# Layer 1 of a two-layer AdaLN model in smaller portions per tick, with longer lags, states in three groups and fewer experts summed ahead

## The chip, the cores and the metric

The kernel runs on one core of a Trainium2 chip. The metric is the device time of one execution in microseconds; lower is better. Engines are named as the profile names them: PE (TensorE), DVE (VectorE), ACT (ScalarE), POOL (GpSimd) and SP (SyncE, which here only issues DMAs).

## The reference, cut to what matters

Eight batches of 512 tokens with 128 channels pass through two blocks. Each half of a block normalises the tokens, scales and shifts them by a vector per batch, applies a sublayer and adds its gated result to `x`.

```python
h = layernorm(x) * (1 + ca0) + sa0;  x = x + ga0 * attention(h)          # Layer 0: 16 heads of 8
h = layernorm(x) * (1 + cb0) + sb0;  x = x + gb0 * moe(h)                # 8 experts 128-512-128, top 2, and a shared one
h = layernorm(x) * (1 + ca1) + sa1;  x = x + ga1 * ssm(h)                # Layer 1, first half
h = layernorm(x) * (1 + cb1) + sb1;  x = x + gb1 * ffn(h)                # Layer 1, second half

def ssm(x):            # 16 states
    xc = conv(x, 4 taps along tokens, per channel) + conv_b
    delta, B_in, C = split(xc @ Win + b_in)          # B_in and C: means of pairs
    A = -exp(A_log);  dA = softplus(delta) * A;  A_bar = exp(dA)
    B_bar = (A_bar - 1) / A * B_in                   # a Taylor form where A is tiny
    h = scan(h * A_bar + B_bar along tokens)
    return (C * h) @ Wout + b_out

def ffn(x):
    x1 = x + silu(pointwise(conv(x, 3 taps)) + pw_b)
    rw = softmax weights of the top 2 of x1 @ router
    combined = sum over 8 experts of rw[e] * silu(x1 @ expert_w[e] + expert_b[e])
    h = rmsnorm(x1 + combined @ out_w + out_b) * norm_w
    return h + gelu(h @ down) @ up
```

## The kernel before, in words

All data are float32; one matmul of the program is two passes on PE. `x` of each batch stays in SBUF as `xs[b]`, 128 tokens on partitions by four chunks (`NC4`).

**Attention** runs in half-ticks called slots (`slot(s)`), with other work hung on slots by `at_slot`. Layer 0's tokens are scattered to DRAM rows sorted by expert (`x_rows`) while attention runs.

**Layer 0's experts** run in a loop of `n = 62` ticks, one block of 256 rows a tick: 31 routed blocks of batches 0-5, 12 blocks of the shared expert, 15 routed blocks of batches 6-7, 4 shared ones. In tick i the loop does `turn_in` of block i+1 (PE transposes, DVE copies to `xt`), `up` of block i (`ph`, L943, then four Gelus on ACT), `down` of block i-1 (`pyb`, L954), and the fetches of blocks ahead: rows `xg` and first weights `w1b` three blocks ahead (`fetch`), second weights `w2b` two ahead (`fetch_2`). Results go to DRAM (`y_rows`).

**Layer 1** is a list of events: `when(t, do, ...)` appends a call to tick t, and a tick's calls are issued in the order in which they were appended. Events of ticks below n run inside the expert loop, after that tick's block; the ticks from n on have no blocks, and follow one another. All engines but PE's matmuls inside a helper are wrapped so that they keep program order, and PE's matmuls are pinned too, so every engine executes in the order in which the ticks issue.

Per batch, the first half of Layer 1 consists of: `gather` (16 indirect DMAs on POOL fetch a batch's two expert results per token in pieces, L974), `combine` (DVE adds them by gate, adds to `xs[b]`, and takes statistics), `ssm_root` (a power on POOL), `ssm_centre` (DVE ends the root, ACT writes the centred tokens `xh`, POOL adds a bias row to `xs[b]`), `ssm_channels` (PE transposes `ptn`, L1107, ACT scales), `ssm_conv` (DVE, into `xc`, two buffers). `ssm_project(h, s)` brings two batches' states on 32 partitions (`pj`, L1146); `chain_1` to `chain_4` compute the softplus, the exponentials and the scan for a group of batches at once, with 16 partitions per batch; `ssm_out` brings them back (`py`, L1214).

Before the change there are two groups of four batches. Batches 0-5 take these steps in ticks 36-51, inside the loop; group 0's chain has ticks 48-53. Batches 6 and 7 take them in ticks n+1 to n+8, and group 1's chain starts at n+10.

The second half begins with the lead-in of a batch, 12 calls from `ssm_out` to `ffn_gates_out`: statistics, root, centre, channels, `ffn_pointwise` (`pw`, L1240, then Silu to `sl`, which shares the two buffers of `xc`), router logits, ranks, gates, and the gates' way to DRAM. From there `ffn_spread` broadcasts them to all partitions (`gb`). Then come eight experts a batch, one a tick: `expert_in` (PE `pe`, L1334, and Silu on ACT to `ye`), three ticks later `expert_gate` (DVE multiplies by the gate into `t`), sums of `t` (two or four by POOL, all eight by DVE in `all_eight`), `expert_sum` (PE multiplies by `out_w`, `r`, L1322). `rms_squares`, `rms_root`, `rms_scale`, `rms_turn` normalise and transpose, `ff_down` and `ff_up` finish for batches 0-3, 4-6 and 7. A batch's first expert is at tick `base[b] = n + 2 + 8b`.

Single-bank PSUM tiles (`bank`) have four buffers, two-bank tiles (`pair`, which `ph` and `r` use) two.

Of the kernel before, what the change touches and what calls it, by code (L numbers as in the profile page):

```python
# [19 lines left out]
P = 128  # L20
# [48 lines left out]
def tile_adaln_two_blocks(  # L69
# [288 lines left out]
    with tc.tile_pool(name="at", bufs=2) as at, tc.tile_pool(name="sc", bufs=4, space=PSUM) as psc, tc.tile_pool(  # L358
# [22 lines left out]
        def load_batch(b, step):  # L381
# [10 lines left out]
            else:  # L392
# [4 lines left out]
                ht = ate.tile([P, S], FP, tag="ht", name="ht", bufs=2)  # L397
# [443 lines left out]
        def routed(h, i):  # L841


            def fetch(it):
# [11 lines left out]
                it["xg"] = fr.tile([P, 2, D], FP, tag="xg", name="xg", bufs=3)  # L856
                Q.dma_start(out=it["xg"], in_=x_rows[h][bass.ds(r, BLK), :].rearrange("(c p) d -> p c d", p=P))
                it["w1"] = fr.tile([P, NF * P], FP, tag="w1b", name="w1b", bufs=3)
                Q.dma_start(out=it["w1"], in_=w1t[:, bass.ds(e, 1), :].rearrange("p o f -> p (o f)"))
# [8 lines left out]
            def turn_in(it):  # L868
                ps = bank("pxt")
                for c in range(2):  # L870
                    pin(T.transpose(ps[:, c, :], it["xg"][:, c, :], ident))  # L871
                it["x"] = fw.tile([P, BLK], FP, tag="xt", name="xt")
                V.tensor_copy(it["x"], flat(ps)[:, 0:BLK])

            def leave(it, py):
# [7 lines left out]
                "fetch": fetch,  # L883
                "fetch_2": fetch_2,
# [6 lines left out]
        def everyone(b, i):  # L891
# [11 lines left out]
            def turn_in(it):  # L903
# [4 lines left out]
                it["gt"] = fw.tile([NE + 1, BLK], FP, tag="gt", name="gt", bufs=3)  # L908
# [15 lines left out]
            def leave(it, py):  # L924
# [5 lines left out]
                "fetch": fetch,  # L930
                "fetch_2": lambda it: None,
# [50 lines left out]
        def combine(b):  # L982
            h, j = home(b)
            acc, yg = shared[b], gathered.pop(b)
            for c in range(NC4):
                n = NC4 * j + c
                for k in range(2):
                    V.scalar_tensor_tensor(
                        acc[:, c, :], yg[:, k, c, :], half[h]["gates"][:, k, n : n + 1], acc[:, c, :], ALU.mult, ALU.add
                    )  # L990
            V.tensor_tensor(acc, acc, sb_rows[:, b : b + 1, :].to_broadcast([P, NC4, D]), ALU.mult)
            V.tensor_tensor(xs[b], xs[b], acc, ALU.add)
            stats(xs[b], mv3, b)
# [78 lines left out]
        def pointwise():  # L1072
# [7 lines left out]
            V.tensor_add(pwb, pp[:, 0:1], col("pw_b"))  # L1080

# [30 lines left out]
        GB = B // 2  # L1112
        GR = 32 * GB // 2

# [3 lines left out]
        def ssm_centre(b):  # L1118
            held["xh", b] = centre(b, mv3, rs3, held.pop(("v3", b)))
            G.tensor_tensor(xs[b], xs[b], gab_rows[:, b : b + 1, :].to_broadcast([P, NC4, D]), ALU.add)  # L1120
# [4 lines left out]
        def ssm_conv(b):  # L1125
            hp, n = held.pop(("hp", b)), S - 1
            xc = lt([P, S], "xc", bufs=2)
            G.memset(xc[:, n:S], 0.0)
            V.tensor_scalar(xc[:, 0:n], hp[:, 0:n], col("conv_w", 0), col("conv_b"), ALU.mult, ALU.add)
            for k in range(1, 4):  # L1130
                V.scalar_tensor_tensor(
                    xc[:, 0:n], hp[:, k : k + n], col("conv_w", k), xc[:, 0:n], ALU.mult, ALU.add
                )
            held["xc", b] = xc

        def ssm_project(h, s):

            if s == 0:
                for name in ("dl", "bi", "ci"):
                    held[name] = lt([GR, S], name)  # L1140
            ps = flat(bank("pj"))
            for i in range(2):
                xc = held.pop(("xc", h * GB + 2 * s + i))
# [13 lines left out]
        def chained(name, tag=None):  # L1157
            held[name] = lt([GR, S], name, tag=tag)
            return held[name]

        def of_states(name, i=0):
            return k1[name][0:GR, i : i + 1]

        def chain_1(h, step):

            dl = held["dl"]
            if step == 0:
                V.tensor_scalar(dl, dl, of_states("bias"), None, ALU.add)
                u = chained("u")
                V.scalar_tensor_tensor(u, dl, -1.0, dl, ALU.mult, ALU.min)  # L1170
            else:
                u = held["u"]
                A.activation(u, u, AF.Exp)
                A.activation(u, u, AF.Ln, bias=ones[0:GR, 0:1])

        def chain_2(h, step):
            dl, u = held["dl"], held["u"]
            if step == 0:
                V.scalar_tensor_tensor(dl, dl, 0.0, u, ALU.max, ALU.add)
                da = chained("da")  # L1180
                G.tensor_scalar(da, dl, of_states("asm"), None, ALU.mult)
# [442 lines left out]
```

## Time and profile before

| | us |
|---|---|
| shown runs | 1134.63, 1137.09, 1138.1; median 1137.09 |
| the profiled execution | 1118.58 |
| its span, first to last instruction | 1116.8 |
| busy in the span: PE, DVE, ACT, POOL | 1011.5, 650.7, 635.9, 475.6 |
| mean granted PE clock | 0.939 of full speed |

The profile is one execution; its time is below the shown runs. A row of the profile's groups names the line, the engine, the tile written and the tiles read, the shape, the count, the busy time and the mean duration, and the idle time just before these instructions with what ended it. Most DVE, ACT and POOL instructions have line 65, that of the wrapper which keeps their order, so they are told apart by tile names.

### The profile page before, as it was taken

How to read it: one execution, taken by the hardware profiler on the slowest of the kernel's cores; microseconds unless marked ns; L12 is line 12 of the kernel's file. 1: busy time of each engine (PE TensorE's matmuls, PEld its weight loads, DVE VectorE, ACT ScalarE, POOL GpSimd, SP SyncE). 2: the span in 40 equal slices, each digit the busy share in tenths (PEclk: the TensorE clock that was granted, in tenths of full speed). 3: DMA queues.
4: the chain of work that ended last, by engine and by line, in shares of the span. 5: the costliest groups of instructions: out<-in, count | busy, mean ns of one | idle time of the engine just before them, and what ended most of it. 6: DMA issues, size and time to landing. Idle time of an engine off the chain costs nothing.

```text
span 1116.8 us, 23956 instructions
## 1 busy us (share of the span) xinstructions
PE 1011.5 (91%) x9420; PEld 652.9 (58%) x9420; DVE 650.7 (58%) x1346; ACT 635.9 (57%) x1376; POOL 475.6 (43%) x727
## 2 busy tenths in 40 slices
PE   6799999999999999999989999997899656766877
PEld 6255555555555555555579999885786523433545
DVE  4377776776777777776521023276762676576463
ACT  2156666666776667676745565453767445434543
POOL 4401223362644546352462033586323745544450
PEclk9589999999999999999999999998999966878899
DMA  9960000000000000000056677413550222211341
GB/s 305 284 175 2 3 1 12 1 28 4 16 17 9 23 2 30 1 25 7 16 157 201 179 205 217 137 42 95 151 151 25 80 93 82 68 59 58 118 128 38
DMA packets 92031, 90.58 MB, mean 81 GB/s; under 512 B 6768, under 2 KB 71352, under 8 KB 91920
## 3 DMA queue, kind: packets, MB, share of 16 engines
q1 hardware_dynamic: 86928, 78.31, 23.5%
q0 software_dynamic: 4688, 9.68, 2.9%
q8 instruction: 74, 1.21, 0.4%
q10 hardware_dynamic: 304, 1.08, 0.3%
q14 instruction: 37, 0.30, 0.1%
HBM read 57.71 MB, written 31.33 MB: 80 GB/s over the span
## 4 chain that ended last, share of the span: by engine, by line
PE 72%; DVE 9%; POOL 8%; ACT 4%; issue 4%; DMA 3%; SPq 0%; POOLq 0%; DVEq 0%; ACTq 0%
PE ps L474 21%; PE av L495 11%; PE pyb L954 8%; PE ph L943 8%; PE pm L446 4%; PE pw L1240 2%; POOL yg L974 2%; POOL t L65 2%; PE pmt L462 2%; PE ppt L513 1%; PE pqk L406 1%; PE pe L1334 1%; DMA x_rows<-tok,ux 1%; DVE t L65 1%; DVE var L65 1%
## 5 line engine op out<-in xcount | busy, mean ns | idle before, releaser
L65 DVE TENSOR_REDUCE mpad<-pm 128x2 f32<-128x1024 f32 x256 | 309.8, 1221 | 137.0 <-PE pm L446 123.3
L65 ACT ACTIVATE es<-ps 128x512 f32<-128x512 f32 x512 | 275.4, 598 | 164.5 <-PE pm L446 117.2
L474 PE MATMUL ps<-qt,kt 32*128 32x512 f32 x1024 | 292.0, 635 | 0.1
L446 PE MATMUL pm<-kt,qt 32*128 32x512 f32 x1024 | 280.0, 664 | 4.5 <-POOL kt L65 2.4
L495 PEld LDWEIGHTS av<-es,vaug 128*32 128x32 f32 x4096 | 104.2, 109 | 94.1 <-ACT part L65 42.5
L495 PE MATMUL av<-es,vaug 128*32 128x128 f32 x4096 | 137.7, 276 | 0.0
L474 PEld LDWEIGHTS ps<-qt,kt 32*128 32x128 f32 x1024 | 94.4, 185 | 60.9 <-issue 31.7
L65 ACT ACTIVATE hid<-ph,bias 128x256 f32<-128x256 f32 x184 | 72.3, 477 | 70.2 <-PE ph L943 70.1
L943 PE MATMUL ph<-xt,w1b 128*128 128x256 f32 x368 | 92.1, 395 | 7.4 <-DVE xt L65 7.4
L708 POOL DMA_INDIRECT x_rows<-tok,ux x64 | 64.5, 1007 | 73.5 <-DMA x_rows<-tok,ux 65.3
L954 PEld LDWEIGHTS pyb<-w2b,hid 128*128 128x128 f32 x736 | 91.6, 195 | 5.2 <-ACT hid L65 2.3
L446 PEld LDWEIGHTS pm<-kt,qt 32*128 32x128 f32 x1024 | 79.7, 190 | 25.1 <-DVE mpad L65 11.4
L954 PE MATMUL pyb<-w2b,hid 128*128 128x128 f32 x736 | 92.3, 279 | 1.7 <-ACT hid L65 1.7
L65 POOL TENSOR_SCALAR qt<-qf,mask,zero 128x512 f32<-128x512 f32 x32 | 24.6, 768 | 149.9 <-PE pm L446 128.5
L1334 PE MATMUL pe<-x,l1w_sb 128*128 128x512 f32 x128 | 76.1, 718 | 4.4 <-ACT ye L65 4.4
L943 PEld LDWEIGHTS ph<-xt,w1b 128*128 128x128 f32 x368 | 69.4, 199 | 16.7 <-DVE xt L65 8.3
L65 POOL TENSOR_TENSOR t<-t 128x512 f32<-128x512 f32 x42 | 60.9, 1449 | 42.0 <-DVE t L65 40.9
L974 POOL DMA_INDIRECT yg<-y_rows,yrows x64 | 63.3, 988 | 33.7 <-issue 17.8
L65 ACT ACTIVATE ye<-pe,pc 128x512 f32<-128x512 f32 x64 | 43.1, 685 | 49.2 <-PE pe L1334 48.8
L65 DVE COPY xt<-pxt 128x256 f32<-128x256 f32 x46 | 19.3, 419 | 84.2 <-PE pxt L871 84.0
L1107 PE MATMUL ptn<-ident,xh 128*128 128x128 f32 x64 | 16.7, 355 | 34.7 <-ACT xh L65 34.4
L65 DVE TENSOR_TENSOR t<-ye,gb 128x512 f32<-128x512 f32 x64 | 43.8, 709 | 0.0
(315 smaller groups left out, 1502.3 us busy)
## 6 DMA issues: line engine op xcount, KB each, us to landing
x_rows<-zeros SPq DMA_DIRECT2D x16, 1024.0 KB, 10.6
gb<-g_rows SPq DMA_DIRECT2D x32, 512.0 KB, 4.9
w1b<-in_w1t SPq DMA_DIRECT2D x46, 256.0 KB, 3.0
w2b<-in_w2t SPq DMA_DIRECT2D x46, 256.0 KB, 3.5
xg<-x_rows SPq DMA_DIRECT2D x46, 128.0 KB, 3.0
y_rows<-yb SPq DMA_DIRECT2D x46, 128.0 KB, 2.5
x<-in_x SPq DMA_DIRECT2D x8, 256.0 KB, 6.5
h_chan<-hf SPq DMA_DIRECT2D x8, 256.0 KB
```

The lines of the kernel that those rows point to most:

```text
L65: return lambda *args, **kwargs: self.pin(call(*args, **kwargs))
L446: T.matmul(pm[:, i, :], lhsT=qt[r : r + 32, qc * P : (qc + 1) * P], rhs=kt[r : r + 32, :], start=True, stop=True,)
L462: pin(T.transpose(pt[:, c, :], mpads[g % 4][:, c, :], ident))
L474: T.matmul(ps, lhsT=kt[r : r + 32, kc * P : (kc + 1) * P], rhs=qt[r : r + 32, :], start=True, stop=True)
L495: T.matmul(ps[32 * j : 32 * j + 32, 0, :], lhsT=vaugs[b % 2][:, kc, 4 * j + m, :], rhs=es_of[4 * g + kc, j][:, q], start=(kc == 0), stop=( ...
L708: nc.gpsimd.indirect_dma_start(out=x_rows[h], out_offset=IndirectOffsetOnAxis(ap=chosen["ux", b][:, k, c : c + 1], axis=0), in_=half[h]["t ...
L943: pin(T.matmul(ph[:, f, :], lhsT=it["w1"][:, f * P : (f + 1) * P], rhs=it["x"], start=True, stop=True))
L954: T.matmul(py[:, c, :], lhsT=it["hid"][:, f, c * P : (c + 1) * P], rhs=it["w2"][:, f, :], start=(f == 0 and "shared" not in it), stop=(f = ...
L974: nc.gpsimd.indirect_dma_start(out=gathered[b][:, k, c, :], out_offset=None, in_=y_rows[h], in_offset=IndirectOffsetOnAxis(ap=half[h]["yro ...
L1107: pin(T.transpose(pt[:, c, :], xh[:, c, :], ident))
L1240: pin(T.matmul(pw, lhsT=k1["pwk"][:, t, :], rhs=hq[:, t : t + S], start=(t == 0), stop=(t == 2)))
L1334: pin(T.matmul(pe, lhsT=l1w_sb[:, 2 + e, :], rhs=x1s[b], start=True, stop=True))
```

## The change

The loop's fetches reach further: rows four blocks ahead, first weights three (a call of their own, `fetch_1`), second weights two, all after `down`; `turn_in` runs two blocks ahead. Layer 1's steps are cut up (`combine` in five portions, statistics in two, convolution in two, `chain_3` in two, the bias additions on their own), and the events stand further apart: up to n a tick is taken as 4.0 us and afterwards as 2.2 us, and each step of a lead-in has a lag in us. The states go in groups of batches 0-3, 4-5 and 6-7. Experts are summed by two for batches 0-3, by four for 4-6 and not at all for 7 before PE takes them; `all_eight` goes. In batches 0-3 `ffn_pointwise` forms Silu from Tanh. Within a tick the experts' calls now stand ahead of the lead-ins' and of the states'.

```diff
-                ht = ate.tile([P, S], FP, tag="ht", name="ht", bufs=2)
+                ht = ate.tile([P, S], FP, tag="ht", name="ht")
...
-                it["xg"] = fr.tile([P, 2, D], FP, tag="xg", name="xg", bufs=3)
+                it["xg"] = fr.tile([P, 2, D], FP, tag="xg", name="xg", bufs=4)
...
-                it["x"] = fw.tile([P, BLK], FP, tag="xt", name="xt")
+                it["x"] = fw.tile([P, BLK], FP, tag="xt", name="xt", bufs=3)
...
+        def two_stats(b, mv, i):
+            for c in (2 * i, 2 * i + 1):
+                st = stat.tile([P, 6], FP, tag="bnst", name="bnst")
+                V.bn_stats(st, xs[b][:, c, :])
+                V.bn_aggr(mv[:, b * NC4 + c, :], st)
...
-        GB = B // 2
-        GR = 32 * GB // 2
+        GROUPS = ((0, 1, 2, 3), (4, 5), (6, 7))
...
-            A.activation(sl, pw, AF.Silu, bias=k1["pwb"])
+            if b in GROUPS[0]:
+
+                th = lt([P, S], "th", tag="gt1", bufs=2)
+                A.activation(th, pw, AF.Tanh, bias=k1["pwb2"], scale=0.5)
+                V.tensor_scalar(sl, pw, k1["pwb"], 0.5, ALU.add, ALU.mult)
+                V.scalar_tensor_tensor(sl, th, 1.0, sl, ALU.add, ALU.mult)
+            else:
+                A.activation(sl, pw, AF.Silu, bias=k1["pwb"])
...
-        def sums_before(b):
-
-            return b < B - 1
+        def sums_of(b):
+
+            return 2 if b < 4 else 4 if b < B - 1 else 1
...
-            if sums_before(b):
-
-                n = 1
-                while n < 4 and (e + 1) % (2 * n) == 0:
-                    G.tensor_tensor(t, f.pop(("t", e - n)), t, ALU.add)
-                    n *= 2
-
-        def all_eight(b):
-            V.tensor_tensor(ffn[b]["t", NE - 1], ffn[b].pop(("t", 3)), ffn[b]["t", NE - 1], ALU.add)
+            n = 1
+            while 2 * n <= sums_of(b) and (e + 1) % (2 * n) == 0:
+                G.tensor_tensor(t, f.pop(("t", e - n)), t, ALU.add)
+                n *= 2
...
+        def later(t, us):
+            while us > 0:
+                us -= 4.0 if t < n else 2.2
+                t += 1
+            return t
+
+        def chain(h, t, lags):
+            steps = ((chain_1, 0), (chain_1, 1), (chain_2, 0), (chain_2, 1), (chain_3, 0), (chain_3, 1), (chain_4,))
+            for (do, *args), i in zip(steps, lags):
+                when(t + i, do, h, *args)
+
+        def lead_in(b, t):
+
+            when(t, ssm_out, b)
+            for i in range(2):
+                when(later(t, 2 * i + 1) if t >= n else t, two_stats, b, mv4, i)
+            for do, us in (
+                (ffn_root, 4), (ffn_centre, 8), (ffn_channels, 12), (ffn_pointwise, 16), (ffn_logits, 22),
+                (ffn_ranks, 24), (ffn_chosen, 28), (ffn_tanh, 30), (ffn_gates, 32), (ffn_gates_out, 36),
+            ):
+                when(later(t, us), do, b)
+
+        base = [n + 5 + NE * b for b in range(B)]
+        for b in range(B):
+            t = base[b]
+            for e in range(NE):
+                when(t + e, expert_in, b, e)
+        for b in range(B):
+            t = base[b]
+            for e in range(NE):
+                when(t + e + 3, expert_gate, b, e)
...
+            every = sums_of(b)
+            lag = 4 if every == 1 else 5 if every == 2 else 6
+            when(t + every - 1 + lag, sum_begin, b)
+            for e in range(every - 1, NE, every):
+                when(t + e + lag, expert_sum, b, e)
+            late = t + NE - 1 + lag
+            when(late + 1, rms_squares, b)
+            when(late + 2, rms_root, b)
+            when(late + (4 if b < last else 3), rms_scale, b)
+            when(late + (6 if b < last else 4), rms_turn, b)
...
-        for b, t in enumerate((36, 38, 40, 42, 45, 47)):
-            for i, do in enumerate(normal):
-                when(t + i, do, b)
+        for b, ts in enumerate(
+            (
+                (36, 37, 38, 39, 40, 41, 47),
+                (38, 39, 40, 41, 42, 43, 48),
+                (41, 42, 43, 44, 45, 46, 49),
+                (43, 44, 45, 46, 47, 48, 50),
+                (46, 47, 48, 49, 50, 51, 52),
+                (49, 50, 51, 52, 53, 54, 55),
+            )
+        ):
...
-        when(47, ssm_project, 0, 1)
-        when(40, out_weights, 0)
-        chain(0, 48, 1)
-        when(56, ssm_project, 1, 0)
...
+        when(49, ssm_project, 0, 1)
+        when(53, out_weights, 0)
+        chain(0, 50, (0, 0, 1, 2, 3, 3, 4))
+        for b in GROUPS[0]:
+            lead_in(b, 55 + b)
+        when(59, ssm_project, 1, 0)
...
+        when(n, out_weights, 1)
+        chain(1, n, (0, 1, 2, 4, 6, 7, 8))
+        lead_in(4, n + 10)
+        lead_in(5, n + 13)
         for b, t in ((6, n + 1), (7, n + 4)):
...
+            for c in range(NC4):
+                when(t + c, combine, b, c)
+            when(t + 4, combine, b, NC4)
+            for i in range(2):
+                when(t + 5 + i, two_stats, b, mv3, i)
+                when(t + 12 + i, ssm_conv, b, i)
+            when(t + 7, ssm_root, b)
+            when(t + 9, ssm_centre, b)
+            when(t + 10, ssm_bias, b)
+            when(t + 11, ssm_channels, b)
+        when(n + 16, out_weights, 2)
+        when(n + 19, ssm_project, 2, 0)
+        chain(2, n + 20, (0, 1, 2, 4, 6, 7, 8))
+        lead_in(6, n + 30)
+        lead_in(7, n + 37)
...
-        at_slot(LAST - 3, lambda: work[0]["fetch"](work[0]))
...
+        ahead = ("fetch", 4), ("fetch_1", 3), ("fetch_2", 2)
...
+        work[0]["turn_in"](work[0])
+        work[1]["turn_in"](work[1])
...
+            if i + 2 < n:
+                work[i + 2]["turn_in"](work[i + 2])
```

## Prediction

> **What bounds it now.** I read the page's first two parts, then the table of stretches, then the waits, then the timeline at the longest wait. The page's busy totals and the row of TensorE slices come first:
>
> ```profile
> PE 1011.5 (91%) x9420; PEld 652.9 (58%) x9420; DVE 650.7 (58%) x1346; ACT 635.9 (57%) x1376; POOL 475.6 (43%) x727
> ...
> PE   6799999999999999999989999997899656766877
> ...
> PEclk9589999999999999999999999998999966878899
> ```
>
> TensorE is full from the third slice to the 27th (attention, then Layer 0's expert blocks). That part is TensorE's own work and the change leaves it alone. The holes are in the last 13 slices, Layer 1. I cut these at tick boundaries, found from the block matmuls (`ph`) and from `x1b`, which runs once per batch, eight ticks apart. The stretches are about ticks 36-53, 54-61, 62-74, 75-91, 92-107, 108-119 and 120 to the end. (The first two rows together are ticks 36-53. Columns: us, then busy PE, PE load, DVE, ACT, POOL, then granted clock, DMA.)
>
> ```profile
> 721.00:754.00 33.00, 33.00 (x221) 28.54 (x221) 24.46 (x78) 18.03 (x45) 26.84 (x31) 1.00 0.19 51
> 754.00:823.00 69.00, 56.96 (x333) 46.90 (x332) 46.20 (x117) 41.39 (x89) 31.25 (x44) 0.88 0.45 125
> 823.00:878.00 55.00, 54.69 (x336) 43.00 (x334) 20.66 (x88) 33.71 (x72) 19.57 (x22) 1.00 0.21 61
> 878.00:933.00 55.00, 27.40 (x94) 13.06 (x92) 34.89 (x90) 29.30 (x47) 32.41 (x38) 0.78 0.29 103
> 933.00:999.00 66.00, 49.91 (x156) 26.91 (x157) 44.46 (x114) 25.13 (x58) 33.16 (x30) 0.70 0.17 56
> 999.00:1043.00 44.00, 29.89 (x99) 14.88 (x97) 31.08 (x72) 19.73 (x46) 23.94 (x19) 0.87 0.33 102
> 1043.00:1076.00 33.00, 31.40 (x144) 18.70 (x143) 15.50 (x31) 18.62 (x39) 16.38 (x12) 0.97 0.44 137
> 1076.00:1117.00 41.00, 29.78 (x178) 21.52 (x176) 17.16 (x47) 12.61 (x31) 7.93 (x7) 0.95 0.13 39
> ```
>
> From 878 to 1043 us no engine is full (DVE 63 to 71%) and the clock is at its worst. The waits of 880-1117 name a ring, not one engine:
>
> ```profile
> ACT ye L65 <- PE pe L1334: 48.8, 34, 6.6
> POOL t L65 <- DVE t L65: 40.9, 16, 4.7
> PEld ptn L1107 <- ACT xh L65: 38.8, 20, 12.0
> ACT xh L65 <- DVE nm L65: 31.9, 6, 8.3
> ```
>
> The 12.0 us wait, in the timeline:
>
> ```profile
> 890.62 0.29 DVE L65 TENSOR_SCALAR var<-mv_l1a 128x4 f32<-128x4 f32 x1
> ...
> 894.68 1.05 POOL L65 TENSOR_TENSOR rstd_l1a<-var,mhalf 128x4 f32<-128x4 f32 x1
> 895.76 0.36 DVE L65 TENSOR_TENSOR var<-var,rstd_l1a 128x4 f32<-128x4 f32 x2 [4.84 <-POOL rstd_l1a L65]
> ...
> 896.75 1.65 ACT L65 ACTIVATE xh<-x,nm,rstd_l1a 128x128 f32<-128x128 f32 x4 [8.26 <-DVE nm L65]
> 897.29 0.18 PEld L1107 LDWEIGHTS ptn<-ident,xh 128*128 128x128 f32 x1 [12.04 <-ACT xh L65]
> ```
>
> The root of batch 6 queues behind gathers on POOL. DVE waits for it with the next combine behind it, and PE waits at the transposes with ready expert matmuls behind them. Root, centre and transpose stand in successive ticks, so a late engine stops all.
>
> A sum supports this. For each tick I multiplied its instructions by their row durations (expert matmul pair 0.86 us, gate 0.67, POOL add 1.45, combine 0.43 a piece and so on, PE at full clock) and took the fullest engine of the tick. Added over ticks 62 to the end this makes **236 us**; the profile has 239 (878 to 1117). So Layer 1 runs in lock step: each tick costs its fullest engine, and the lags absorb nothing.
>
> **The skill.** Three places bear on it. "Perfetto Trace Analysis", section Tensor Engine Instruction, says ACT, DVE and GPSIMD are strict FIFO; the stack-up above agrees. "TensorE: Matmul & The Clock Gate", Part 1, says that PE falls to half clock after an idle window of about 3.4 us; the trace agrees, since the expert passes after the 12 us wait are 0.86 us apart and those of a full queue 0.43. "ScalarE: Activation LUTs", What ACT_TABLE_LOAD costs, gives about 1283 ns a load; the row's mean is 1283 ns.
>
> **The change, part by part.**
>
> *Ticks 36-53.* The same work for batches 0-5, in single-tick portions: combine pieces, combine end with statistics, root, centre, channels, convolution, bias. The worst DVE tick falls from 10.9 to 7.7 us by my sum. `turn_in` moves two blocks ahead (`xt` 3 buffers, `xg` fetched four ahead), so DVE may fall a further tick (about 4 us) behind before `ph` waits, as it does now ("ph <- DVE xt", 7.4 us in the stretch 728-880). `ssm_bias` (1.3 us POOL, which waited on ACT ahead of gathers) goes to tick 47 and later, `out_weights` to 53. Measured 102 us; PE's floor is 81 (DVE 72, POOL 63). Lock step gives 100. I take 90: **-12**, between -21 and -2.
>
> *Ticks 54-61.* Lead-ins of batches 0-3 spread out; one `pw` and most of `pl` and `pgt` slide past tick 62, PE 55.1 to 49.9. The four Silu become Tanh plus two DVE passes (0.58 and 0.76 us, from the `xc` rows): DVE +5.4 us over four ticks where it is under 40% busy; four table loads (5.1 us ACT) go, because `z`'s Tanh at 878 needed none after a Gelu. **-5**, between -7 and 0.
>
> *States in 4, 2, 2.* One chain more: DVE 0.47+0.68+0.68+0.48+0.68+0.74+1.21+0.74, that is 5.7 us; POOL 4.2; ACT 2.1 and four or five loads, 5.1 to 6.4. The instructions don't shorten with fewer partitions. In return batches 4 and 5 don't wait for 6 and 7, and the lags of 1 to 2 ticks take the chain out of successive ticks. Its cost is inside the sums below.
>
> *Experts by two or four.* Batches 0-3 go from one summed tile to four, 4-6 to two: three extra sets of 8 passes for four batches and one for three, 15 sets at 0.99 us (eight passes of 0.124 in the chain): PE **+15 us**. POOL loses 8 adds of 1.45 (-11.6), DVE seven `all_eight` (-4.8), and the wait DVE-POOL-DVE-PE at each batch's end goes with it.
>
> *Ticks 62 to the end.* Summed anew, PE goes from 130 to 151 us and DVE from 131 to 139; ACT 106 to 114, POOL 114 to 115. Per stretch the fullest engine has: 62-74 DVE 37.7; 75-91 DVE 38.8 (PE 36.9); 92-107 PE 31.2; 108-119 PE 29.6. In lock step they take 50.1, 55.5, 42.2, 33.3. Most dependent steps now follow two or more ticks later and the expert instructions stand first in each tick, so a late root no longer stops PE at once. I choose near the middle: 43, 47, 37 and 32, against 55, 66, 44 and 33: **-39**. The experts start at n+5 instead of n+2 and the closing chain is as serial as before: the last stretch 45 against 41, **+4**.
>
> *A new wait.* `sl` shares the two `xc` buffers. Batch 4's Silu stands in tick 80 but both are held until `ssm_project(2,0)` in tick 81. ACT then waits for PE's tick 81 (0.86+0.99+0.5+0.95 = 3.3 us) with `ye` queued behind. Between 0 (PE ahead) and 3.3; batch 0 has the same within tick 59. Taken as **+2** together.
>
> *At nothing.* `ht` with one buffer: a batch's values are read six slots (some 12 us: attention has 264 slots in about 520 us) before the next is written. SP now issues each `y_rows` write ahead of that tick's fetches, so they wait for `yb`, about 2.4 us; `w1b` lands in 3.0 and has two ticks. If that cover went, a block would wait at most those 2.4. Fetches start a slot earlier in attention; no gain is taken. The memsets are the same.
>
> Sum: -12 -5 -39 +4 +2 = **-50**. The profiled execution took 1118.58 us, of which 1.8 lie around its span; that makes 1069. The shown runs' median is 18.5 us higher, and no view says where. I carry the difference over: 1137.1 - 50 = **1087**.
>
> **The rivals.**
>
> *Lock step remains* (20%). If a late engine still stops the others, the tail saves only 236 - 226 = 10 us of its tick sums, 13 against the measured 239. With 2 to 5 us in the loop that is **1119 to 1122**. For it: before's tail fits lock step within 3 us, and PSUM's four single banks bound how far PE runs ahead. Against: before's steps had one tick of lag, these have two or more.
>
> *Nearly free flow* (15%). The fullest engine bounds each stretch: 37.7+38.8+31.2+29.6+45 = 182, -57; loop -26. That is **1054**. Against it: DVE would have to be above 95% busy through 30 ticks.
>
> *Slower: a cold TensorE* (9%). PE now has 20 us more work after tick 62. If lock step remains and the idle gaps keep PE at half clock, doubling PE's time in the tick sums makes 318 before and 337 after, +19; less some 8 of the loop, **1148**. It decides where the tail's clock stays under about 0.7 (tick sums 265 and 268 there, even). The 0.70 of 933-999 speaks for it; against it, PE's gaps are the very thing the lags shorten.
>
> *The portions don't move* because the scheduler orders them otherwise (3%): the pinned program order speaks against it; about 1137.
>
> **Numbers.** Forecast, lags half working: 53%, 1087, own range 1070 to 1108. With the rivals, eight in ten lie in **1060 to 1122**. A difference within 0.3%, 3.4 us, is about what can't be told from no change: 5%, the unmoved case and a little of lock step; faster 86%, slower 9%.
>
> **What would show it.** Right: DVE at 80% or more in ticks 62-91, tail clock at 0.9 or above, "ptn <- xh" waits under 10 us in total, `r<-l1w_sb,t` x240 with some 15 us more busy time, x34 POOL adds. Wrong: a tail of over 225 us, a clock still near 0.7, or a new long wait at `sl` or at a PSUM bank.

## The result, and the profile after

After the change the kernel took **1123.29 us** (median; 1122.73 to 1124.82) beside 1137.59 for the kernel before in the same set of runs: ratio 0.9873, interval 0.984 to 0.9907, 14.3 us or 1.3% faster. Forecast was 1087, range 1060 to 1122: the right direction, but the gain was far too large. The page after, in the same rows as before:

```profile
PE 1024.6 (91%) x9540; PEld 668.8 (60%) x9540; DVE 665.2 (59%) x1356; ACT 634.2 (56%) x1378; POOL 470.6 (42%) x723
...
PE   5799999999999999999989999859889957878987
...
PEclk9689999999999999999989999969989977889899
```

Two things show. The holes at the end are shallower than before, and there is a new one in the middle (the 8 and the 5 of the PE row), where PE had been full. The timeline of PE there (TensorE's matmuls of the shared expert, tick 34; in brackets the idle time and its cause):

```profile
722.31 0.71 PE L917 MATMUL pyb<-b_sb,gt 9*128 9x128 f32 x4
722.95 0.38 PE L958 MATMUL pyb<-ws,hid 128*128 128x128 f32 x1
723.56 0.27 PE L958 MATMUL pyb<-ws,hid 128*128 128x128 f32 x1 [0.24 <-issue]
724.27 0.37 PE L958 MATMUL pyb<-ws,hid 128*128 128x128 f32 x1 [0.44 <-issue]
724.99 0.27 PE L958 MATMUL pyb<-ws,hid 128*128 128x128 f32 x1 [0.34 <-issue]
727.09 0.50 PE L958 MATMUL pyb<-ws,hid 128*128 128x128 f32 x3 [1.83 <-issue]
```

From 723 to 745 us PE gets its instructions 0.70 us apart (or twice that) and waits on "issue", that is on nothing the profile shows. The tick takes 25.5 us instead of 4.6. I call this **the stretch**. Every time below needs one sentence on it: in some sets of runs every profile taken has it, of before and of after alike, and in others none has. The chip does not decide it: the record gives the same chip for sets 1 and 4.

| set | before | stretch | other kernels of the set |
|---|---|---|---|
| the shown runs | 1137.59 | in the profile of after | after 1123.29 |
| 1 | 1136.91 | yes | before_again, loop_only, sums_four, leads_late |
| 2 | 1118.5 | no | straight_rows, ranks_dve, chain_late, handover |
| 3 | 1137.91 | yes | after_again, dve_relief, pool_relief, best |
| 4 | 1119.48 | no | straight_rows_b, rank_hand, spread_gathers, both_relief |
| 5 | 1117.33 | no | straight_rows_c, after_third |

Before's first profile (1118.58) has no stretch: that is most of the difference of 18.5 us to its shown runs which the prediction could not place. Times are compared within one kind of set only.

**Where the time went, without the stretch.** Before's first profile against that of after_third (span 1090.4 us, set 5). A tick is dated by its block's first `hid`; "handed over" is from the 505th of attention's 512 `es` to the first `hid`. All in us.

| part | before | after | predicted change | measured |
|---|---|---|---|---|
| up to that `es` | 554.0 | 552.9 | 0 | -1.1 |
| handed over to the loop | 20.4 | 23.4 | 0 | +3.0 |
| ticks 0-35 | 149.0 | 148.9 | 0 | -0.1 |
| ticks 36-53 | 101.8 | 90.0 | -12 | -11.8 |
| ticks 54-60 | 50.4 | 44.2 | -5 | -6.2 |
| tick 61 to the end | 241.2 | 230.9 | -33 | -10.3 |
| span | 1116.8 | 1090.4 | -50 | -26.4 |

The tail holds nearly the whole miss. Its waits in after_third (engine, tile, whom it waited for; us, times, longest):

```profile
ACT ye L65 <- PE pe L1374: 31.7, 24, 3.8
ACT xh L65 <- DVE nm L65: 24.0, 5, 6.0
POOL t L65 <- DVE t L65: 21.3, 9, 6.3
...
PEld r L1362 <- POOL t L65: 14.8, 11, 3.3
PE pgt L1336 <- DVE gate L65: 14.4, 4, 6.7
...
PEld ptn L1126 <- ACT xh L65: 10.0, 17, 3.3
...
DVE rk_gt L65 <- POOL rk_eq L65: 7.0, 2, 3.9
```

The 38.8 us of `ptn` behind `xh` are down to 10.0 and the longest from 12.0 to 3.3: a late root no longer stops PE for long. In its place two waits have grown that were short in the kernel before: `pgt` for `gate` from 2.4 to 14.4 us, `rk_gt` for `rk_eq` from 2.5 to 7.0.

### The profile page after: what moved, and what is told of

Its sections match the earlier page's. It is cut to its first block, busy times and chain, and to the rows that moved or that the text cites. A ratio compares the mean times of both kernels' runs of the same rounds, so it can differ in the third digit from the quotient of the medians.

```text
span 1123.0 us, 24186 instructions
## 1 busy us (share of the span) xinstructions
PE 1024.6 (91%) x9540; PEld 668.8 (60%) x9540; DVE 665.2 (59%) x1356; ACT 634.2 (56%) x1378; POOL 470.6 (42%) x723
## 5 line engine op out<-in xcount | busy, mean ns | idle before, releaser
L474 PEld LDWEIGHTS ps<-qt,kt 32*128 32x128 f32 x1024 | 95.3, 185 | 61.1 <-issue 33.3
L65 ACT ACTIVATE hid<-ph,bias 128x256 f32<-128x256 f32 x184 | 72.3, 478 | 57.6 <-PE ph L947 53.6
L65 POOL TENSOR_SCALAR qt<-qf,mask,zero 128x512 f32<-128x512 f32 x32 | 24.7, 773 | 149.0 <-PE pm L446 128.7
L1374 PE MATMUL pe<-x,l1w_sb 128*128 128x512 f32 x128 | 73.1, 680 | 0.5 <-ACT ye L65 0.4
L65 POOL TENSOR_TENSOR t<-t 128x512 f32<-128x512 f32 x34 | 49.3, 1451 | 36.2 <-DVE t L65 23.8
L65 DVE TENSOR_TENSOR t<-ye,gb 128x512 f32<-128x512 f32 x64 | 53.2, 848 | 4.6 <-POOL t L65 4.6
L958 PE MATMUL pyb<-ws,hid 128*128 128x128 f32 x256 | 36.2, 287 | 12.5 <-issue 12.5
```

Source lines behind the costliest of these rows:

```text
L65: return lambda *args, **kwargs: self.pin(call(*args, **kwargs))
L474: T.matmul(ps, lhsT=kt[r : r + 32, kc * P : (kc + 1) * P], rhs=qt[r : r + 32, :], start=True, stop=True)
L958: T.matmul(py[:, c, :], lhsT=it["hid"][:, f, c * P : (c + 1) * P], rhs=it["w2"][:, f, :], start=(f == 0 and "shared" not in it), stop=(f = ...
L1374: pin(T.matmul(pe, lhsT=l1w_sb[:, 2 + e, :], rhs=x1s[b], start=True, stop=True))
```

## The experiments

Theories: **H**, a stall of TensorE's supply of instructions (the stretch) splits the runs into two kinds. **L**, later **Q**: at the tail's start POOL's queue holds up the short rank steps, and with them VectorE and TensorE. **D**: VectorE itself is what ticks 62-91 have too little of. **P**: TensorE's added expert passes are paid. **A** and **B**: the loop or the tail carries the gain. G, S, O and T are explained in the expectations that use them. "Tail" is tick 61 to the end; a **lap** is the time from one `x1b` to the next (there is one per batch, eight ticks apart).

### Is before also of two kinds? (before_again: before, unchanged)

> The kernel before, unchanged, profiled once more. Its profiled execution took 1118.58 us, its other runs 1134 to 1142. Theory H (a hole in TensorE's instruction supply): in the profile of after TensorE gets one instruction every 0.7 us between 722.95 and 745.4 us, 20 us lost; the runs of before at about 1137 contain such a hole somewhere and its first profiled execution did not. Then a profile at about 1137 shows one stretch of 16 to 23 us in which TensorE waits on "issue" before every instruction, and all else is as in the first profile to within 2 us. Rival: the 18 us are spread over the span (slower transfers, slower clock); then every stage is 1 to 2 per cent longer and no such stretch exists.

1137.16 us. Its profile (span 1131.2) has the stretch, in tick 34, 719.8 to 733.8 us:

```profile
721.25 0.33 PE L954 MATMUL pyb<-ws,hid 128*128 128x128 f32 x1 [1.06 <-issue]
722.65 0.57 PE L954 MATMUL pyb<-ws,hid 128*128 128x128 f32 x1 [1.07 <-issue]
724.03 0.37 PE L954 MATMUL pyb<-ws,hid 128*128 128x128 f32 x1 [0.82 <-issue]
725.43 0.37 PE L954 MATMUL pyb<-ws,hid 128*128 128x128 f32 x1 [1.03 <-issue]
```

Ticks 31-35 take 38.1 us instead of 22.0, all other parts agree with the first profile within 1.8 us. H holds: the 16.1 us lie in the 16 to 23 that it expected.

### After in both kinds of set (after_again, after_third: after, unchanged)

> After, unchanged, profiled once more. In the second set of runs the kernel before took 1118.5 us without a hole in tick 34 and four small variants of after 1090 to 1093, also without one; in the first set before took 1137 and after's variants 1123, all with the hole. If the set is one without the hole: 1089 to 1093, that is 25 to 29 us less than before, ticks 36 to 53 91 us (before 101.8), 54 to 61 44 us (50.4), the tail 229 to 231 us (241.2). If with it: 1122 to 1125.

> After, unchanged. In a set without the stretch in tick 34: 1088 to 1093 against before's 1118 to 1120, 27 to 30 us less, ticks 36 to 53 90 to 91 us, 54 to 61 44.2, the tail 229 to 233. In a set with it: 1121 to 1125 against 1137.

With the stretch 1121.9 us (ratio 0.986, 0.9818 to 0.9902); without it **1093.18 us, ratio 0.9786, 0.9764 to 0.9808**. So the change gives 24 us without the stretch, about half of the 50 forecast, and 14 to 16 with it. The trace of after_again says where the rest goes: ticks 31-35 take 43.6 us (before_again 38.1), and ticks 36-53 97.1 instead of 90.0, with one tick of 11.0 in which PE waits on "issue" again, for 1.06 us, and the next at a clock of 0.60 (both ticks are the same in the first profile of after). Before_again lost nothing there (101.5).

### Do POOL's gathers cause the stretch? (straight_rows, _b, _c)

```diff
+            if h == 0:
+                m = P * (8 * j + n)
+                Q.dma_start(out=gathered[b][:, k, c, :], in_=y_rows[h][m : m + P, :])
+                return
             pin(nc.gpsimd.indirect_dma_start(
```

The lookup of each token's rows is left out for batches 0 to 5: their rows come in storage order.

> After, with the 48 gathers of batches 0 to 5 (POOL, indirect, 1.25 us each) replaced by plain transfers of 128 rows in order from SyncE's queue: the values of Layer 0's routed experts go to wrong tokens, everything else is computed as before. TensorE's instruction stream is unchanged. So far all five profiles with a hole have it at tick 34, 14 to 20 us long, while POOL issues gathers back to back. Theory G (the stream of gathers starves TensorE's instruction supply): no hole, tick 34 takes 4.6 us, the time falls by 16 to 22 us to 1101 to 1107. Theory S (the hole comes from TensorE's own instruction stream at that place): hole and time stay, 1119 to 1124.

Two repeats, in sets 4 and 5, put the same two theories to the test. The three took 1090.4, 1088.76 and 1089.68 us, without a stretch; but all three fell into sets in which the kernel before had none either. They tell nothing of its cause, which stays open. They show something else: with the gathers gone from POOL, ticks 36-53 take 86.6 us instead of 90.0, so the gathers cost some 3.4 us there.

### The loop's portions alone (loop_only)

After's loop, with before's groups, sums and Silu, and its lags in the lead-ins (`lead_early` takes them as before, root one tick on to gates out nine ticks on):

```diff
-        GROUPS = ((0, 1, 2, 3), (4, 5), (6, 7))
+        GROUPS = ((0, 1, 2, 3), (4, 5, 6, 7))
...
-            lead_in(b, 55 + b)
+            lead_early(b, 54 + b // 2)
...
-        base = [n + 5 + NE * b for b in range(B)]
+        base = [n + 2 + NE * b for b in range(B)]
```

> After's block loop (portions per tick for batches 0 to 5, turn_in two ahead, split fetches) with before's tail: states by 4 and 4, before's lags of the lead-ins, experts from n+2 summed by eight (by one in batch 7), Silu. Theory A (most of the gain is in the loop: ticks 36 to 61 were 13 us shorter in the profile of after, its hole left out, the tail 5 us): 1122 to 1127. Theory B (the hole hid what the loop gives, and the tail carries half or more of the 14 us): 1129 to 1136. If the instruction hole falls away or doubles with the new instruction order, the time shifts by some 20 us and the profile shows it; then the stretches are compared without it.

1136.58 us, ratio 1.0006 (0.999 to 1.0022): nothing. Against before_again its trace has 2.4 us more at the handover, 3.0 more in ticks 31-35, 3.5 less in 36-53, 6.1 more in 54-60 and 6.8 less in the tail. That is just above B's range of 1129 to 1136 and far from A's; but the set has the stretch, which hides part of the loop's gain, so this run does not say how large that gain is. The 6.1 us look like the variant's own: in tick 54 the scan and `ssm_out` meet (PE waits 4.64 us for `ci`) while VectorE has 9.5 us of work. From tick 54 to the end it takes 290.1 us, before_again 290.7, after_again 277.1: with before's lags and sums behind them the loop's portions gain nothing there. What they would give in a set without the stretch was not measured.

### TensorE's added passes (sums_four)

```diff
-            return 2 if b < 4 else 4 if b < B - 1 else 1
+            return 4 if b < B - 1 else 1
```

> After, with the experts of batches 0 to 3 summed by four instead of by two: 8 sets of 8 TensorE passes less (8 x 0.99 = 7.9 us of TensorE), 8 POOL adds of 1.45 us more, nothing else. Theory P (TensorE's added passes are paid in the tail): 5 to 8 us faster, 1115 to 1118. Theory D (VectorE bounds ticks 62 to 91, TensorE's passes lie beside it): within 2 us, 1121 to 1125. Theory O (POOL work slows VectorE's gate multiplications, whose mean grew from 709 to 848 ns): slower by 2 to 6 us, and the gates' mean rises above 848 ns.

1123.22 us; tail 233.9 us against 232.9 in after_again. Eight of the fifteen added sets of passes are gone, and nothing is gained: P falls, at least for this exchange of TensorE's passes for eight additions on POOL. The lap between the sixth and seventh `x1b` shrinks from 27.2 to 21.7 us, the others grow by as much in all. O falls too: with eight more additions on POOL the gates' mean fell from 848 to 806 ns.

### The tail's start: five variants

leads_late moves logits to gates of batches 1-3; ranks_dve moves one product; chain_late delays the second chain:

```diff
+                if 1 <= b < 4 and us >= 22:
+                    i = {22: 0, 24: 1, 28: 3, 30: 4, 32: 5, 36: 7}[us]
+                    when(n + 5 + NE * b - 11 + i, do, b)
...
-            G.tensor_tensor(eq, eq, tri.unsqueeze(1).to_broadcast(shape), ALU.mult)
+            V.tensor_tensor(eq, eq, tri.unsqueeze(1).to_broadcast(shape), ALU.mult)
...
-        chain(1, n, (0, 1, 2, 4, 6, 7, 8))
+        chain(1, n + 6, (0, 1, 2, 4, 6, 7, 8))
```

> After, with the logits, ranks, choice, tanh, gates and their store of batches 1, 2 and 3 moved from ticks 62 to 72 to the eleven ticks ahead of each batch's first expert (ticks 64, 72, 80 on). Theory L (these short steps, behind POOL's gathers, hold up TensorE and VectorE at the tail's start: waits of gate transposes 14.2 us, of ranks 7.0, experts 12 us later than before): 5 to 12 us faster, 1111 to 1118, and the wait of pgt for gate falls under 5 us. Theory D (VectorE is full in ticks 62 to 91 whatever the order): within 3 us, 1120 to 1126.

> After, with Layer 1's product rk_eq x tri on VectorE (about 0.4 us) instead of POOL (0.7 us). In the profile of after and in the run with the late lead-ins, rk_eq waits on POOL behind gathers and the second chain (8.3 us in one place, 7.0 in the other), VectorE's rk_gt waits for it with everything behind, and TensorE's gate transposes wait 14 to 18 us with ready experts behind. Theory Q (POOL's queue holds up the tail's start): the wait rk_gt for rk_eq goes, pgt for gate falls under 6 us, and the tail is 5 to 9 us shorter: 1114 to 1118. Theory D (VectorE is what bounds ticks 62 to 91; 8 x 0.4 us more of it): 0 to 4 us slower.

> After, with the second chain (batches 4 and 5) from tick n+6 instead of n, and the lead-ins of batches 4 and 5 from n+16 and n+18 instead of n+10 and n+13. Nothing is added. Theory Q (in ticks 62 to 70 POOL's da and ts of this chain, 4.2 us, stand between the gathers and the rank products of batches 1 to 3): 3 to 6 us faster, 1117 to 1120. Theory D (the same work only moves into ticks in which VectorE is already full): within 2 us or slower by up to 4.

leads_late: 1122.65 us, tail 234.5. The wait of `pgt` did not fall, it rose to 18.3 us, because a rank product still met the queue. POOL's timeline of this run shows it (gathers, then the second chain, then the product), and VectorE's next step:

```profile
910.69 0.94 POOL L978 DMA_INDIRECT yg<-y_rows,yrows  x1 [0.30 <-issue]
911.68 1.57 POOL L65 TENSOR_SCALAR da<-dl,asm 32x512 f32<-32x512 f32 x1
913.34 0.61 POOL L65 TENSOR_SCALAR ts<-da 32x512 f32<-32x512 f32 x1
914.04 1.25 POOL L65 TENSOR_TENSOR ts<-ts,da 32x512 f32<-32x512 f32 x1
915.39 0.69 POOL L65 TENSOR_SCALAR ts<-ts,small 32x512 f32<-32x512 f32 x1
916.05 0.71 POOL L65 TENSOR_TENSOR rk_eq<-rk_eq,tri 128x256 f32<-128x256 f32 x1
...
916.80 0.42 DVE L65 TENSOR_TENSOR rk_gt<-rk_gt,rk_eq 128x256 f32<-128x256 f32 x1 [8.27 <-POOL rk_eq L65]
```

ranks_dve: 1091.2 us (set 2), tail 227.2 against after_third's 230.9; `pgt` for `gate` falls from 14.4 to 9.4 us. The 3.7 us are fewer than the 5 to 9 that Q expected, and they are not safe as a gain in the tail. In seven profiles whose tail is that of after (after, after_again, after_third, handover and the three with straight rows) the tail is anything from 228.9 to 232.9 us, mostly because the third lap is anything from 25.6 to 29.7; and rank_hand below, which moves the same product, has a tail of 229.2 beside handover's 228.9. The first lap is steady, 33.0 to 33.8 in the seven, and it falls to 29.5 in ranks_dve and 30.5 in rank_hand. So Q is right for the first lap, by about 3 us. chain_late: 1092.53, tail 230.2: nothing, as D expected and against Q's 3 to 6 us.

The reliefs leave work out for batches 6 and 7. dve_relief leaves out the additions of the routed rows in `combine` and three of the four taps of `ssm_conv`, as below; pool_relief the lookup of rows, with the straight rows shown above under `if h == 1`; both_relief all of it.

```diff
-                for k in range(2):
+                for k in range(2 if b < 6 else 0):
...
-                if k > 0:
+                if k > 0 and b < 6:
```

> After, leaving out on VectorE, for batches 6 and 7 alone, the sixteen additions of the routed experts' rows (x 0.4 us) and three of the four taps of the convolution (six x 0.8 us): 11 us of VectorE in ticks 63 to 78. All other instructions are there. Theory D (VectorE bounds ticks 62 to 91): the tail is 7 to 11 us shorter. Theory Q (what counts there is the chain of short steps through POOL's queue): 0 to 4 us shorter.

> After, with the 16 gathers of batches 6 and 7 (POOL, 1.25 us each) replaced by plain transfers of 128 rows in order from SyncE's queue: the values of Layer 0's routed experts go to wrong tokens for these two batches. POOL has 20 us less in ticks 60 to 68. Theory Q (POOL's gathers hold up the rank products): the tail is 5 to 9 us shorter, the waits of rk_gt for rk_eq go, pgt for gate falls under 6 us. Theory D: within 2 us.

> After with both reliefs: plain transfers instead of the gathers of batches 6 and 7 (wrong tokens), and without their sixteen additions of routed rows and three of four convolution taps. Alone the tails were 223.1 and 226.9 us against 232.9. If the two causes are separate and add: 217 +- 1.5. If both only shorten the same wait: 222 to 224. If a third bound lies close below (TensorE's ring with the experts): 220 to 222.

dve_relief 1117.87, pool_relief 1115.75 us (set 3), both_relief 1081.71 (set 4). Tails: 226.9, 223.1 and 220.1 us, against 232.9 (set 3) and 230.9 (set 5) of after. dve_relief's 6.0 us lie between the theories (D 7 to 11, Q 0 to 4), pool_relief's 9.8 above Q's 5 to 9. The laps between the first four `x1b`, in after_third, then pool_relief, then both_relief (us; busy PE, PE load, DVE, ACT, POOL; clock, DMA):

```profile
876.57:909.65 33.08, 18.32 (x56) 9.36 (x54) 24.84 (x74) 11.41 (x22) 18.91 (x19) 0.70 0.36 115
909.65:938.21 28.56, 23.86 (x95) 12.48 (x94) 23.60 (x52) 16.48 (x39) 16.68 (x22) 0.88 0.29 91
938.21:966.04 27.83, 22.48 (x86) 13.82 (x86) 21.58 (x41) 17.63 (x31) 16.46 (x15) 0.75 0.11 39
```

```profile
907.90:935.31 27.41, 17.94 (x55) 9.65 (x55) 26.16 (x76) 11.62 (x22) 10.86 (x10) 0.66 0.37 120
935.31:963.62 28.31, 23.07 (x96) 12.18 (x94) 23.39 (x51) 16.34 (x38) 16.43 (x21) 0.94 0.27 91
963.62:989.39 25.77, 18.65 (x86) 12.08 (x86) 21.22 (x40) 17.62 (x31) 16.10 (x15) 0.87 0.12 42
```

```profile
876.91:901.23 24.32, 16.95 (x55) 9.70 (x54) 23.07 (x61) 11.42 (x23) 11.53 (x10) 0.74 0.44 146
901.23:926.10 24.87, 21.63 (x96) 11.50 (x94) 18.73 (x44) 16.34 (x38) 15.83 (x21) 1.00 0.29 93
926.10:955.62 29.52, 24.17 (x86) 15.21 (x86) 20.86 (x41) 17.64 (x31) 16.23 (x15) 0.71 0.12 36
```

In the first lap POOL's gathers decide: without them 27.4 us instead of 33.1 (33.8 in after_again), and now VectorE is busy in 26.2 of them, 95%. The wait of `rk_gt` is gone, that of `pgt` for `gate` falls from 14.1 us in after_again to 8.6, not under the 6 expected. (The plain transfers also bring the rows at other times; what that is worth was not measured apart.) With VectorE relieved as well, the lap takes 24.3. Over the first two laps the reliefs add, and a little more: 61.6 us in after_third and after_again, 55.7 in pool_relief, 57.6 in dve_relief, 49.2 with both. So both causes are shown for these two laps. The third lap, which has the same work in all of them, takes 25.8 to 29.5 us, no more and no less than in the kernels with after's own tail. So of pool_relief's 9.8 us in the tail the 3.9 of the third lap may not be its doing, and both_relief's 220.1, which lies in the range expected if a third bound lay close below, does not show one. The third lap goes with the clock (0.87 and 0.71, the same 86 matmuls taking 18.7 and 24.2 us); what sends it one way or the other I did not settle.

### The first blocks (handover)

```diff
-        work[1]["turn_in"](work[1])
...
-            if i + 2 < n:
+            if i + 2 < n and i > 0:
                 work[i + 2]["turn_in"](work[i + 2])
             if i < n:
                 up(work[i])
+            if i == 0:
+                work[1]["turn_in"](work[1])
+                work[2]["turn_in"](work[2])
```

> After, with only the first block turned in ahead of the first up, and blocks 1 and 2 directly behind it (before turned in one block ahead throughout). In the traces of after and its variants the first hid comes 23.3 to 23.5 us after the last attention blocks (es at 553 us), in those of before 20.4 to 20.9: TensorE waits at the third transposition for the rows of blocks 1 and 2. Theory T (two turn_ins ahead of the first up cost it): that stretch falls to 20.4 to 21, 2.5 to 3 us less in all. Rival (the order of the first fetches costs it: the rows of four blocks now stand ahead of the second weights): it stays above 22.5.

The first `hid` comes 16.7 us after that `es`, not 23.4; but tick 10 stands only 1.8 us earlier (62.3 instead of 64.1), as blocks 1 and 2 wait for their rows now. T expected 2.5 to 3. The time is 1091.46 us. PE in after_third, where three transpositions wait for rows ahead of the first `ph`:

```profile
565.88 0.41 PE L873 MATMUL pxt<-ident,xg 128*128 128x128 f32 x2 [1.38 <-DMA xg<-x_rows]
569.80 0.66 PE L873 MATMUL pxt<-ident,xg 128*128 128x128 f32 x2 [3.51 <-DMA xg<-x_rows]
570.26 1.06 PE L526 MATMUL pot<-ident,o 128*128 128x128 f32 x4
572.47 0.66 PE L873 MATMUL pxt<-ident,xg 128*128 128x128 f32 x2 [1.16 <-DMA xg<-x_rows]
572.92 3.31 PE L947 MATMUL ph<-xt,w1b 128*128 128x256 f32 x8
```

### Versions that keep all the work (best, rank_hand, spread_gathers)

best has ranks_dve, handover, chain_late (with the lead-ins of batches 4 and 5 at n+16 and n+18) and leads_late; rank_hand only the first two; spread_gathers has rank_hand and

```diff
-            when(n - 2 + k // 3, gather, PB[0] + k // 8, k % 8)
+            when(n - 2 + (3 * k) // 5, gather, PB[0] + k // 8, k % 8)
...
-        for b, t in ((6, n + 1), (7, n + 4)):
+        for b, t in ((6, n + 4), (7, n + 8)):
```

with the third chain three ticks later and its lead-ins two.

> After with four changes together: Layer 1's rank product on VectorE (alone, the tail measured 227.2 us against 228.9 to 230.3 in the other variants of its set), only one block turned in ahead of the first up (alone, the loop's tick 10 came 1.8 us earlier), the second chain and the lead-ins of batches 4 and 5 six and five ticks later, and the gates of batches 1 to 3 in the eleven ticks ahead of their experts. Theory Q and D together (waits at the tail's start go, and VectorE's work is spread over ticks in which it has room): 6 to 10 us faster than after. Theory D alone (VectorE's sum decides): 2 to 4 us faster, what the first block brings.

> After with two changes: Layer 1's rank product on VectorE, and only one block turned in ahead of the first up. In their own runs the tail's lap between the first two x1b was 29.5 us instead of 33.2 to 33.8, and the loop came 1.8 us earlier. Theory Q: 4 to 6 us faster than after, tail 227. Rival (the next late engine takes it back): 0 to 2.

> The kernel with rank product and first block changed, and besides the 16 gathers of batches 6 and 7 spread over ticks 60 to 69 (five in three ticks instead of three in one), their combines from n+4 and n+8 instead of n+1 and n+4, and the third chain three ticks later. Theory Q (POOL's queue, full of gathers, holds up roots, ranks and chain): a further 2 to 5 us faster than with the two changes alone. Theory D (VectorE's sum counts, and its work only moves): within 2 us of it.

best: 1122.43 us beside after's 1121.9: nothing; its first lap takes 37.2 us. **rank_hand: 1087.93 us, ratio 0.9721 (0.969 to 0.9751); spread_gathers: 1087.49, 0.9725 (0.9697 to 0.9753).** After's own ratio without the stretch is 0.9786 (0.9764 to 0.9808), so both beat both kernels, after by some 0.6%; the comparison goes by way of before, as after did not run in set 4. rank_hand's tail of 229.2 is not the 227 that Q expected. Spreading takes the first lap down to 21.8 us, and the next two up to 32.4 and 30.2: the time is within 2 us of rank_hand's, as D said, and not 2 to 5 better, as Q said.

## Why the prediction was right or wrong

- **Ticks 36-53, -12:** right, -11.8, where the stretch is absent. The worst ticks of before (11.0, 9.4 and 10.0 us, ticks 42-44) are gone, none takes over 7.8 now, and so is the wait that the forecast named. It stood in before and does not occur in after_third in these ticks:

```profile
PE ph L943 <- DVE xt L65: 7.4, 3, 4.5
```

  Which portion or lag earns how much was not tested apart.
- **Ticks 54-61, -5:** right, -6.2.
- **"At nothing":** wrong for one edit. `ht` and the queue of SP cost nothing (attention is the same); but turning in two blocks ahead of the first `up` makes PE wait for the rows of three blocks, +3.0 (handover takes 1.8 of it back). I had priced the fetches of the loop's steady state, not its start.
- **Experts by two or four:** PE's row `r` has +16.9 us for the +15 forecast, POOL's additions -11.3 for -11.6. Sized right; whether PE's share is paid is open, as giving eight of the fifteen sets back to POOL changed nothing (sums_four).
- **The lags' effect on PE:** right. `ptn` waits are what was forecast (10.0 us at most), and the clock of the tail rose from 0.83 to 0.88, just short of the 0.9 named. VectorE is busy in 79% of ticks 62-91, where 80% was named.
- **The tail, -39:** the step that failed is "I choose near the middle": the longer lags were to save about half of what lies between lock step and free flow. None of that saving shows. From tick 62 to the end after_third takes 228.5 us where before took 239; the lock step sums, with the 45 forecast for the last stretch, made 226. By the ticks of `x1b`, with those between two of them taken as equal, ticks 62-74 take about 51 us (forecast 43, lock step 50.1), 75-91 about 58 (47, 55.5), 92-107 about 42 (37, 42.2), 108-119 about 33 (32, 33.3), the rest 45 as forecast. The sign that I had named for being wrong, a tail of over 225 us, came true. Two reasons are shown for part of it. First, I made tick sums per engine and asked which is fullest; I did not ask what stands ahead of what in POOL's queue once the lead-ins had slid past tick 62: sixteen gathers, the second chain, and behind them rank products of 0.7 us that VectorE and PE wait for. Taking the gathers away made the tail 9.8 us shorter, 6.4 of them in the first lap. Second, VectorE's sum: I had 139 us from tick 62 to the end, the trace has 159.8. Before's was short too (131 against 143.1), so some of that is the row means I used. The lock step sums fit although they hold the same too small durations, so the fit alone does not prove lock step. Another part the change itself makes (the first line is of before, the others of after_third):

```profile
L65 DVE TENSOR_TENSOR t<-ye,gb 128x512 f32<-128x512 f32 x64 | 43.8, 709 | 0.0
L65 DVE TENSOR_TENSOR t<-ye,gb 128x512 f32<-128x512 f32 x64 | 53.2, 848 | 4.6 <-POOL t L65 4.6
L65 POOL TENSOR_TENSOR t<-t 128x512 f32<-128x512 f32 x34 | 49.6, 1459 | 36.2 <-DVE t L65 21.3 <-PE ph L1421 5.4 <-DVE z L65 3.2
L1362 PE MATMUL r<-l1w_sb,t 128*128 128x128 f32 x240 | 33.9, 287 | 12.4 <-POOL t L65 7.1 <-POOL hq L65 2.1 <-DVE t L65 1.8
```

  The 64 gates have the same shape as before and take 53.2 us instead of 43.8. In after_again 13 of them take 1.50 us in the mean, the others 0.68. All 13 start inside a POOL operation, as this one of after_third does:

```profile
959.09 1.30 POOL L65 TENSOR_TENSOR t<-t 128x512 f32<-128x512 f32 x1 [0.70 <-DVE z L65]
959.18 1.76 DVE L65 TENSOR_TENSOR t<-ye,gb 128x512 f32<-128x512 f32 x1
```

  POOL ends at 960.39 and the gate, begun at 959.18, 0.55 us later; so do the other twelve, 0.55 us after POOL's end. The Trainium skill, "SBUF — State Buffer", section SBUF: two separate sides, states just this: a VectorE operation with two SBUF inputs and a GpSimd operation that reads SBUF take a shared pair of ports in turn, each for its whole instruction. The trace agrees, and in both directions: 18 more gates start inside a POOL record and keep 0.68 us. In nine of these cases POOL has less than 0.3 us left, in the other nine POOL's operation is the one that grows (an addition of `t` to 2.6 us, from 1.26). In the new order 13 gates are held up instead of 2. What these 9.4 us of VectorE cost the tail was not tested apart; sums_four and chain_late have 9 slow gates and a tail no shorter to speak of.

  Both reasons together do not make up the 22.7 us: with the gathers and 11 us of VectorE's work left out (both_relief) the tail is still 220.1 us, beside the 208 that the forecast amounts to. Why the longer lags let so little flow stays open beyond that.
- **The closing chain, +4, and the wait at `sl`, +2:** the last ticks are about as forecast. `sl` (here VectorE's) waited 6.0 us for `pj`, in tick 59, where PE is busy throughout, so it probably cost nothing; in tick 80 there was no such wait.
- **Carried over to the median:** it held for before, but by luck: its 18.5 us are mostly the stretch (16.1 us in the trace of before_again), which the profile behind the forecast did not have. After loses 30 us with it (1093.18 against 1123.29). Those 11.6 us more, the tail's 22.7 and the handover's 3.0, less 1.2 of ticks 54-60, come to 36.1 of the miss of 36.3.
- **The rivals:** "lock step remains" gave 1119 to 1122. In the number it stands nearest, which is partly luck, as the stretch, which it knew nothing of, is in the 1123.29. In the tail it was right: it took 10 to 13 us off there, and some 10 went. In the loop it was wrong, with 2 to 5 us where 18 went (ticks 36-60). The long waits at `ptn` did go; a queue and a nearly full VectorE are part of what took their place.

## What to carry to other kernels

When steps are spread over ticks, redo the queue of every in-order engine in its new order, not only its sum: in leads_late a 0.7 us product behind six gathers and a chain held VectorE for 8.3 us, and TensorE's gate transposes with it. Relieving the fullest ticks moves work into the next ones, so look at what those have left before pricing the gain. And where a profile's own time is off the runs by more than their spread, profile again before carrying the difference over: here most of it was a stall that the changed kernel paid more for. And before a tail that is some us shorter in one profile is called a gain, see how far it moves between profiles of kernels that do the same there: here 4 us.

## What the runs showed of the hardware

- TensorE can be down to one instruction per 0.70 us, or per twice that, for 14 to 22 us, while the profile shows nothing that it waits for. It came at the same tick in all kernels, in whole sets of runs or not at all. In the profile of after the DMA queues of kind "instruction" moved no packet from 716 to 755 us, around the stretch of 723 to 745; in those of before and after_third one came between 715 and 735. So late instructions are likely, but not shown to be the cause. In the profiles of before_again and after POOL issued gathers back to back meanwhile, but it does so without the stretch too.
- A VectorE multiplication of two 128x512 operands takes 0.68 us alone. In after_again 13 of the 31 that start inside a POOL operation take 1.16 to 1.77 us and end 0.55 us after it; the others keep 0.68, with POOL's operation at its end or drawn out instead.
- The same 86 matmuls of the third lap took 18.7 us at a mean granted clock of 0.87 in pool_relief and 24.2 us at 0.71 in both_relief.
